# A recommendation kernel's first and last stretch: where rows are fetched, and which units run on column groups

## The chip, the core and the metric

The kernel runs on one core of a Trainium2 chip. A core has five engines that run side by side, each with its own queue of instructions: TensorE (PE, matrix products into PSUM), VectorE (DVE), ScalarE (ACT), GpSimd (POOL) and SyncE (SP, which only issues transfers). Transfers between the device's memory and the on-chip memory (SBUF) are DMAs; SP, ACT and POOL can issue them. The metric is the time of one execution in device microseconds, as the median of three runs. Before the change it is 31,195.79 us (31,191.82 to 31,199.41).

## What is computed

It is a recommender with attention over a history of 200 items for each of 16,384 users. Embedding rows have 64 floats (256 bytes), and the tables have 100,000 rows (users, items) and 1,000 (categories).

```python
u = u_emb[user]; it = i_emb[item]; c = c_emb[cate]
h = i_emb[hist]                                   # 200 x 16384 rows
itb = jnp.broadcast_to(it[None], h.shape)
feat = jnp.concatenate([h, itb, h - itb, h * itb], axis=-1)
a = dice(feat @ au_W1 + au_b1, au_alpha, axis=1)  # 36 units, statistics over the 16384 users
w = a @ au_W2 + au_b2
cur = jnp.sum(w * h, axis=0)
z = jnp.concatenate([u, it, c, cur], axis=-1)
z = dice(z @ W1 + b1, alpha1, axis=0)             # 80 units
z = dice(z @ W2 + b2, alpha2, axis=0)             # 40 units
return z @ W3 + b3                                # 2 outputs
# dice(x): p = sigmoid((x - mean) / sqrt(var + 1e-8)); x * (p + alpha * (1 - p))
```

The history's gather is the bulk: 3.28 million rows.

## The kernel before

The 16,384 users are 128 tiles of 128 (NT), in 8 chunks (ND) of 16 tiles (TD). One history position is therefore 8 steps, and the history 1,600 steps; `step(k)` does one. Five row buffers (`rows`, of 16 tiles each) are used in turn, so POOL may run up to five chunks ahead of DVE, which turns a buffer's rows into columns (`transpose`, L150, L153).

Rows come in one of two ways. `gather` (L124, L125) is an indirect DMA on POOL: one instruction fetches 128 rows by indices. Or "by address": SP or ACT loads row numbers, already multiplied to byte addresses (`load_addresses`, `scale_addresses`), into registers and issues one DMA of 256 bytes for each row (`ask`, L303 to L328, the DMA is L323). These rows land in `side`; `place_tile` (L385) waits for them (`await_rows`) and copies them into the chunk's last tile. Six of the eight chunks have such a tile (SIDES = 1, 3, 4, 5, 6, 7), which leaves 122 tiles to POOL; in two of three history positions chunk 5's is gathered as well.

There are three parts, each in an order written out by hand for every queue (`tc.manual_schedule`).

1. The start (L518 to L567). The items' rows are gathered by `fetch_all`, 122 tiles on POOL, and 768 rows come by address through `ask_all` (L541), 56% on SP and 44% on ACT. Beside it the categories' embeddings are made as a product with one-hot columns: ACT writes the category numbers in another order (`order_categories`, L487, L490), then spreads each half chunk over 125 partitions (`spread_categories`, L496); DVE compares them with eight constants (`pick_categories`, L501, 16 comparisons of 125x1024 a chunk), PE multiplies (L505, two column groups of 64), and ACT copies the product out (L509) and stores it (L516). Chunk 0 is followed by `attention_weights`. At the end of each chunk DVE places the chunk's last tile and transposes the chunk before. `head_weights` (L246 to L279) stands behind it all; of its SP transfers, seven are executed before the loop and the rest after it, as are the DVE operations L274 to L279 that use them.

2. The history: 180 positions in a hardware loop with a body of 90 (L570), then 20 more behind it (`steps`, L638). This part isn't touched.

3. The users' steps and the head (L645 to L675, then L677 to the end). In step j `fetch_all` gathers chunk j of the users' rows, SP loads the chunk's category columns from `catT` (L650), `step` finishes what is left of the history, and `ask_all` (L660) asks for a share of the users' rows by address, for five tiles, half on SP and half on ACT. For chunk c = j - 1 the first layer is computed by parts: category, item, attention (`head_layer`, L617), then the user part (L671) once the rows are transposed. Of the 80 units of this layer, 64 go into `px` with weights `w1a` (two halves of the users fill the 128 partitions), and the other 16 into `ph[:32]` with weights `w1b` (products of 128x32). ACT evacuates both (L623, L631), where L631 moves the 32 partitions to a quarter of `zb`, and `measure_head` (L581) takes statistics. After the last chunk the second layer runs chunk by chunk (L698 to L712): ACT and DVE apply dice, PE adds the product with `w2a` to that of the others with `w2b`, which is computed ahead for four chunks at a time in row groups of 32 (L705, `beside`). The third layer and the output follow.

ACT and SP execute their queues in order, so a row DMA that stands ahead of an activation delays it by its issue.

Of the kernel before, what the change touches and what calls it, by code (L numbers as in the profile page):

```python
# [14 lines left out]
P = 128  # L15
D = 64
# [20 lines left out]
def din_kernel(  # L37
# [76 lines left out]
    ids = [make(f"ids{i}", P, NC, dt=I32) for i in range(2)]  # L114
    side = [make(f"side{i}", P, D) for i in range(3)]
# [117 lines left out]
    w2b = make("w2b", P, P)  # L233
    w3 = make("w3", P, 4, P)
    b1a = make("b1a", P, 1)
    b1b = make("b1b", S, 1)
# [9 lines left out]
    def head_weights():  # L246
# [9 lines left out]
        for g in range(2):  # L256
# [6 lines left out]
            nc.sync.dma_start(b1b[ts(g, ZB)], col(b1)[ZA:])  # L263
            nc.sync.dma_start(bias2[g * ZA : g * ZA + Z2], col(b2))
            nc.sync.dma_start(al2[g * ZA : g * ZA + Z2], col(alpha2))
            for j in range(4):
                r = slice(j * S + g * ZB, j * S + (g + 1) * ZB)
                nc.sync.dma_start(w2b[r, g * ZA : g * ZA + Z2], W2[ZA:])
                w = j * S + g * ZO
                nc.sync.dma_start(w3[g * ZA : g * ZA + Z2, j, w : w + ZO], W3)  # L270
                nc.sync.dma_start(alb[r], col(alpha1)[ZA:])
        nc.sync.dma_start(bias3, b3.partition_broadcast(P))
# [64 lines left out]
    def ask_all(s, split, first, n, at, table):  # L337
        for queue, runs in enumerate(shares(NS * P // ND, s, split)):
            runs = [(r0, min(end, n * P)) for r0, end in runs if r0 < n * P]
            ask(queue, runs, first, range(n), at, table)  # L340

# [47 lines left out]
    def fetch_all(k, c, ids, table):  # L389
        for n in range(TD - (c in SIDES)):  # L390
            j = column(c, n)
            gather(rows[k % ROWS], ids[:, j : j + 1], n, table)
# [91 lines left out]
    def order_categories():  # L484
        for c in range(ND):
            n, j = TD - (c in SIDES), column(c, 0)
            nc.scalar.dma_start(cs[c][:, :n], columns(r_cate)[:, j : j + n])  # L487
            if c in SIDES:
                j = column(c, TD - 1)
                nc.scalar.dma_start(cs[c][:, n:], col(r_cate[j * P : (j + 1) * P]))  # L490
        nc.scalar.dma_start(table, c_emb.rearrange("(b p) d -> p b d", p=PB))
# [26 lines left out]
    with tc.manual_schedule():  # L518
        nc.sync.dma_start(ids[0], columns(r_item))
        load_addresses(2, r_item.rearrange("(o b) -> o b", o=1))  # L520
        nc.vector.memset(hm, 0.0)
        nc.scalar.copy(hT[SPREAD], hm)
        order_categories()
        load_hist_ids(0, 0)
        load_addresses(0, r_hist[0:1])
        nc.sync.dma_start(ids[1], columns(r_user))
        nc.gpsimd.iota(lanes, pattern=[[1, P]], base=P, channel_multiplier=-1)
        for q in range(SPREAD - 1):
            spread_categories(q)
# [4 lines left out]
        scale_addresses(2)  # L534
# [3 lines left out]
        for c in range(ND + 1):  # L538
            if c < ND:
                fetch_all(c, c, ids[0], i_emb)  # L540
                ask_all(c, 0.56, -NS, NS, addr[2], i_emb)  # L541
# [6 lines left out]
            if c == 0:  # L548
                attention_weights()
                scale_addresses(0)  # L550
            if c:
                if c - 1 in SIDES:
                    place_tile(c - 1, SIDES.index(c - 1) - NS)
                transpose(itT[c - 1], rows[(c - 1) % ROWS])
# [12 lines left out]
        head_weights()  # L567
# [10 lines left out]
    zst = [make(f"zst{i}", P, n, STATS) for i, n in enumerate((2 * ND, 4, 2 * ND))]  # L578

    def measure_head(i, j, t, h):  # L580
        nc.vector.bn_stats(zst[i][:, 2 * j + h, :], t[:, ts(h, CH)])  # L581

# [34 lines left out]
    def head_layer(pairs):  # L617
        layer(px, [(w1a[:, f], t) for f, t in pairs], last=False)
        layer(ph[:S], [(w1b[:, f], t) for f, t in pairs], last=False)
# [6 lines left out]
    def head_units(c):  # L626
# [3 lines left out]
        for h in range(2):  # L630
            nc.scalar.activation(  # L631
                zb[c // 4][ts(c % 4, S), ts(h, CH)], ph[:S, ts(h, CH)], AF.Identity, bias=b1b
            )
            if c % 4 == 3:
                measure_head(1, c // 4, zb[c // 4], h)

    with tc.manual_schedule():
        steps(BODY, L - BODY, L - BODY, r_user.rearrange("(o b) -> o b", o=1))  # L638
        U = addr[(L - BODY) % 3]
        j = column(SIDES[-1], TD - 1)  # L640
# [140 lines left out]
```

## Time and profile before

| what | value |
|---|---|
| median of three runs | 31,195.79 us |
| profiled execution | 31,199.79 us |
| its span | 31,198.0 us, 427,397 instructions |
| TensorE clock granted, mean | 0.809 |
| POOL busy | 23,418.8 us (75%), 24,783 instructions |
| PE busy | 20,922.2 us (67%) |
| DVE busy | 15,705.3 us (50%) |
| ACT busy | 3,823.8 us (12%) |
| POOL busy in 0 to 200, 200 to 400 us | 138.6 and 105.4 us |
| POOL busy in 1,000 to 5,000 us | 3,022.9 of 4,000 us |
| PE busy in 30,800 to 31,198 us | 297.0 of 398 us |
| by-address DMAs from the item table, SP and ACT | 68,720 and 68,624 |
| by-address DMAs from the user table, SP and ACT | 336 and 304 |

The span runs from the first to the last recorded instruction; the profiled execution is 1.8 us longer than its span and 4.0 us above the median. Busy time does not count the issue of a DMA by SP or ACT, nor the time between two gathers on POOL, so 75% is not a measure of how free POOL is. An engine's line in a timeline gives the start in us, the duration, the line of the kernel, the operation and its operands; "x16" means that so many like instructions are merged, and brackets hold the wait before the first of them and what ended it. "ACTq" and "SPq" are DMAs that these engines issue.

### The profile page before, as it was taken

What the parts mean: (1) busy time and instruction counts of PE and PEld (TensorE: products, weight loads), DVE (VectorE), ACT (ScalarE), POOL (GpSimd) and SP (SyncE); (2) the same over time, 40 slices, a digit from 0 to 9 for tenths busy, and PEclk for the clock granted to TensorE, in tenths of its full rate; (3) what the DMA queues carried; (4) which work ended last, traced back from release to release, by engine and by line L of the source; (5) the groups of instructions that cost most, each with busy time, mean ns of one, the idle gap of its engine ahead of it and who ended that gap; (6) DMA issues with size and microseconds to landing.
All of it is one profiled execution on the core that took longest, in us unless ns stands there. A gap on an engine that the chain in (4) does not pass through costs nothing.

```text
span 31198.0 us, 427397 instructions
## 1 busy us (share of the span) xinstructions
PE 20922.2 (67%) x39376; PEld 8551.5 (27%) x39376; DVE 15705.3 (50%) x21745; ACT 3823.8 (12%) x3330; POOL 23418.8 (75%) x24783
## 2 busy tenths in 40 slices
PE   5666666666666666666666666666666666666667
PEld 2222222222222222222222222222222222222222
DVE  4555554554555555555455455555555555545554
ACT  1111111111111111111111111111111111111111
POOL 6777777777777777777777777777777777777776
PEclk7888888888888888888888888887888888888888
DMA  2111111111111111111111111111111111111111
GB/s 41 29 29 29 29 29 29 29 29 29 29 29 29 29 29 29 29 29 29 29 29 29 29 29 29 29 29 29 29 29 29 29 29 29 29 29 29 29 29 30
DMA packets 1135469, 907.51 MB, mean 29 GB/s; under 512 B 730704, under 2 KB 730704, under 8 KB 1132426
## 3 DMA queue, kind: packets, MB, share of 16 engines
q0 software_dynamic: 792896, 813.51, 13.9%
q1 hardware_dynamic: 193404, 35.89, 0.8%
q10 hardware_dynamic: 146125, 30.64, 0.7%
q14 instruction: 2734, 22.39, 0.2%
q8 instruction: 310, 5.08, 0.1%
HBM read 873.55 MB, written 4.39 MB: 28 GB/s over the span
## 4 chain that ended last, share of the span: by engine, by line
POOL 32%; issue 12%; PE 5%; DMA 4%; DVE 2%; ACTq 1%; ACT 0%; DVEq 0%; POOLq 0%
POOL rows L125 32%; DMA rows<-in_L_rec_i_emb,idx 4%; PE px L158 2%; PE ph L158 1%; PE wb L158 1%; ACTq L323 1%; DVE hT L153 1%; DVE wb L368 0%; DVE curT L369 0%; ACT pg L361 0%; DVE st L377 0%; ACTq L315 0%; ACT xs L372 0%; DVE y L364 0%; DVE hm L400 0%
## 5 line engine op out<-in xcount | busy, mean ns | idle before, releaser
L125 POOL DMA_INDIRECT rows<-in_L_rec_i_emb,idx x24400 | 23038.6, 944 | 7542.4 <-issue 7198.7
L158 PE MATMUL ph<-hT,unit 128*128 128x512 f32 x6404 | 5928.7, 1077 | 9820.7 <-DVE hT L153 9820.2
L368 DVE SCALAR_TENSOR_TENSOR wb<-wb,au_bias,hT 128x1024 f32<-128x1024 f32 x1609 | 2080.3, 1293 | 9802.6 <-PE wb L158 9802.6
L158 PEld LDWEIGHTS ph<-hT,unit 128*128 128x128 f32 x6404 | 1747.3, 305 | 12865.9 <-DVE hT L153 12687.8
L153 DVE STREAM_TRANSPOSE hT<-rows 64x512 f32<-64x512 f32 x6404 | 4517.0, 705 | 1483.9 <-DMA rows<-in_L_rec_i_emb,idx 894.5
L158 PE MATMUL px<-hT,blk_h 128*128 128x512 f32 x6404 | 4125.0, 733 | 0.0
L372 ACT ACTIVATE xs<-px,au_bias 128x1024 f32<-128x1024 f32 x1602 | 1783.6, 1113 | 14375.2 <-PE wb L158 10720.9
L158 PE MATMUL wb<-y,blk_p 128*128 128x512 f32 x6436 | 3318.4, 597 | 246.6 <-DVE y L364 246.1
L361 ACT ACTIVATE pg<-xs,sh,rs 128x1024 f32<-128x1024 f32 x1609 | 1943.0, 1208 | 12481.6 <-issue 9985.6
L158 PE MATMUL px<-itT,blk_i 128*128 128x512 f32 x6404 | 3355.8, 606 | 0.0
L158 PE MATMUL wb<-xs,blk_x 128*128 128x512 f32 x6436 | 3300.5, 594 | 5.3 <-DVE curT L369 5.3
L158 PE MATMUL px<-hm,blk_m 128*128 128x512 f32 x6408 | 3011.2, 592 | 0.0
L400 DVE TENSOR_TENSOR hm<-ph,itT 128x1024 f32<-128x1024 f32 x1601 | 1960.6, 1225 | 1920.1 <-PE ph L158 1920.0
L364 DVE TENSOR_TENSOR y<-pg,xs 128x1024 f32<-128x1024 f32 x1609 | 1959.4, 1218 | 1293.7 <-ACT pg L361 1291.5
L158 PEld LDWEIGHTS px<-hT,blk_h 128*128 128x128 f32 x6404 | 1649.9, 258 | 2417.9 <-issue 2363.7
L377 DVE BATCH_NORM_STATS2 st<-xs 128x6 f32<-128x512 f32 x3204 | 2058.9, 685 | 60.8 <-ACT xs L372 17.1
L369 DVE TENSOR_TENSOR curT<-wb,curT 128x1024 f32<-128x1024 f32 x1609 | 1970.4, 1225 | 54.8
L158 PEld LDWEIGHTS px<-itT,blk_i 128*128 128x128 f32 x6404 | 1402.0, 219 | 2031.2 <-issue 2031.2
L158 PEld LDWEIGHTS wb<-y,blk_p 128*128 128x128 f32 x6436 | 1215.2, 191 | 1847.9 <-issue 1460.7
L158 PEld LDWEIGHTS wb<-xs,blk_x 128*128 128x128 f32 x6436 | 1224.6, 190 | 1551.9 <-issue 1544.4
L158 PEld LDWEIGHTS px<-hm,blk_m 128*128 128x128 f32 x6408 | 1217.4, 190 | 1532.9 <-issue 1520.3
L387 DVE COPY rows<-side 128x64 f32<-128x64 f32 x1079 | 235.7, 218 | 485.0 <-DMA side<-in_L_rec_i_emb 472.9
(184 smaller groups left out, 2044.3 us busy)
## 6 DMA issues: line engine op xcount, KB each, us to landing
side<-in_L_rec_i_emb SPq DMA_DIRECT2D x68720, 0.2 KB
side<-in_L_rec_i_emb ACTq DMA_DIRECT2D x68624, 0.2 KB
rows<-in_L_rec_i_emb,idx POOLq DMA_INDIRECT x24400
idx<-in_r_hist SPq DMA_DIRECT2D x200, 61.0 KB
hT<-cs ACTq DMA_DIRECT2D x16, 500.0 KB
side<-in_L_rec_u_emb SPq DMA_DIRECT2D x336, 0.2 KB
side<-in_L_rec_u_emb ACTq DMA_DIRECT2D x304, 0.2 KB
ucT<-catT SPq DMA_DIRECT2D x8, 512.0 KB
```

Of the source, the lines that this page charges most:

```text
L125: nc.gpsimd.indirect_dma_start(out=dst[:, n, :], out_offset=None, in_=table, in_offset=bass.IndirectOffsetOnAxis(ap=ids, axis=0),)
L153: nc.vector.transpose(by_tile(dst[ts(e, D)], i)[:, n], of[ts(i, D), n, ts(e, S)])
L158: nc.tensor.matmul(dst[:, ts(i, CH)], lhsT, rhs[:, ts(i, CH)], start=(first and j == 0), stop=(last and j == len(pairs) - 1), skip_group_c ...
L323: dma = issue.dma_start(side[m % 3].bitcast(U8)[p : p + 1], flat[ds(a, ROW)].rearrange("(o d) -> o d", o=1),).then_inc(landed[m % 3], 16)
L361: nc.scalar.activation(pg, xs[k % XR], AF.Sigmoid, bias=shifts[i], scale=rstds[i])
L364: nc.vector.tensor_mul(y, pg, xs[k % XR])
L368: nc.vector.scalar_tensor_tensor(wb, wb, au_bias2, hT[k % LAG], ALU.add, ALU.mult)
L369: nc.vector.tensor_add(curT[k % ND], wb, curT[k % ND])
L372: nc.scalar.activation(xs[k % XR], px, AF.Identity, bias=au_bias)
L377: nc.vector.bn_stats(stats[l % 3][:, 2 * c + i, :], xs[k % XR][:, ts(i, CH)])
L387: nc.vector.tensor_copy(rows[k % ROWS][:, TD - 1], side[m % 3])
L400: nc.vector.tensor_mul(hm, ph, itT[k % ND])
```

## The change

It has four parts.

- All 128 tiles of the items are gathered on POOL. The indices of the six tiles beyond the first 122 get a small tile of their own (`side_ids`, `load_all_ids`). `ask_all` is gone, and with it every by-address DMA of the start.
- ACT's order at the start is changed: the category numbers of three chunks, the table, and then the first spreads between the remaining numbers. `load_hist_ids` and `load_addresses` for the first position come behind `attention_weights`; the users' indices and `head_weights` are put into the third chunk.
- For the users, two tiles (of chunks 3 and 5) come by address, on SP alone, 48 rows a step; the other 126 are gathered. The category and item parts of the first layer are put ahead of a weighing.
- The 16 other units are computed for four quarters of the chunk's columns at once in PSUM, 256 columns each, one quarter for each group of 32 output columns; `zb` is then evacuated by one activation of 128x256, and measured for each chunk. In the second layer `w2b` has two copies, each with zeros for the other quarter, and the others' product of each chunk follows that with `w2a` in two row groups of 64. The bias `b1b` is loaded for all 128 partitions.

```diff
+    def load_all_ids(i, v):
+        for s in range(NS):
+            j = NC + s
+            nc.sync.dma_start(side_ids[i][:, s : s + 1], col(v[j * P : (j + 1) * P]))
-    def fetch_all(k, c, ids, table):
-        for n in range(TD - (c in SIDES)):
+    def fetch_all(k, c, i, table, by_address=()):
+        for n in range(TD):
             j = column(c, n)
-            gather(rows[k % ROWS], ids[:, j : j + 1], n, table)
+            at = ids[i][:, j : j + 1] if j < NC else side_ids[i][:, j - NC : j - NC + 1]
+            if j - NC not in by_address:
+                gather(rows[k % ROWS], at, n, table)
...
         nc.sync.dma_start(ids[0], columns(r_item))
-        load_addresses(2, r_item.rearrange("(o b) -> o b", o=1))
+        load_all_ids(0, r_item)
...
-        order_categories()
-        load_hist_ids(0, 0)
-        load_addresses(0, r_hist[0:1])
-        nc.sync.dma_start(ids[1], columns(r_user))
         nc.gpsimd.iota(lanes, pattern=[[1, P]], base=P, channel_multiplier=-1)
-        for q in range(SPREAD - 1):
-            spread_categories(q)
+        for c in range(3):
+            order_categories(c)
+        nc.scalar.dma_start(table, c_emb.rearrange("(b p) d -> p b d", p=PB))
+        for c in range(3, ND):
+            if c - 3 < SPREAD - 1:
+                spread_categories(c - 3)
+            order_categories(c)
...
-                fetch_all(c, c, ids[0], i_emb)
-                ask_all(c, 0.56, -NS, NS, addr[2], i_emb)
+                fetch_all(c, c, 0, i_emb)
...
             if c == 0:
                 attention_weights()
+                load_hist_ids(0, 0)
+                load_addresses(0, r_hist[0:1])
                 scale_addresses(0)
+            if c == 2:
+                nc.sync.dma_start(ids[1], columns(r_user))
+                load_all_ids(1, r_user)
+                head_weights()
             if c:
-                if c - 1 in SIDES:
-                    place_tile(c - 1, SIDES.index(c - 1) - NS)
                 transpose(itT[c - 1], rows[(c - 1) % ROWS])
...
-        head_weights()
...
+    def others(c):
+        return zb[c // 4][:, ts(c % 4, QH)]
-    def head_layer(pairs):
-        layer(px, [(w1a[:, f], t) for f, t in pairs], last=False)
-        layer(ph[:S], [(w1b[:, f], t) for f, t in pairs], last=False)
+    def head_layer(pairs, first=False, last=False, n=(0, TD)):
+        for i in range(2):
+            for j, (f, t) in enumerate(pairs):
+                nc.tensor.matmul(
+                    by_tile(px, i)[:, slice(*n)], w1a[:, f], by_tile(t, i)[:, slice(*n)],
+                    start=first and j == 0, stop=last, skip_group_check=True,
+                )
+        for j, (f, t) in enumerate(pairs):
+            for r in range(4):
+                n0 = r % 2 * TD // 2
+                of = slice(max(n[0], n0), min(n[1], n0 + TD // 2))
+                if of.start < of.stop:
+                    to = slice(of.start - n0, of.stop - n0)
+                    nc.tensor.matmul(
+                        ph[ts(r, S), :QH].rearrange("p (n t) -> p n t", t=S)[:, to],
+                        w1b[:, f], by_tile(t, r // 2)[:, of],
+                        start=first and j == 0, stop=last, skip_group_check=True,
+                    )
...
-        for h in range(2):
-            nc.scalar.activation(
-                zb[c // 4][ts(c % 4, S), ts(h, CH)], ph[:S, ts(h, CH)], AF.Identity, bias=b1b
-            )
-            if c % 4 == 3:
-                measure_head(1, c // 4, zb[c // 4], h)
+        nc.scalar.activation(others(c), ph[:, :QH], AF.Identity, bias=b1b)
+        nc.vector.bn_stats(zst[1][:, c, :], others(c))
...
+        tiles = [SIDES.index(c) for c in (3, 5)]
-        for j in range(ND + 2):
+        for j in range(ND + 1):
+            c = j - 1
             if j < ND:
-                fetch_all(K + j, j, ids[1], u_emb)
-                if j == SIDES[-1]:
-                    gather(rows[(K + j) % ROWS], sidx[0], TD - 1, u_emb)
+                fetch_all(K + j, j, 1, u_emb, tiles)
                 nc.sync.dma_start(category[j % 2], catT[j])
             step(K + j, K - 1, weighed)
             weighed.add(K + j - LAG)
+            runs = [(r0, r0 + LOAD) for r0 in (2 * LOAD * j, 2 * LOAD * j + LOAD)]
+            runs = [(r0, min(end, len(tiles) * P)) for r0, end in runs if r0 < len(tiles) * P]
+            ask(0, runs, first, tiles, U, u_emb)
+            if j:
+                head_layer(((2, category[c % 2]), (1, itT[c])), first=True)
...
-            if j < ND:
-                ask_all(j, SPLIT, first, NS - 1, U, u_emb)
-            if 1 <= j <= ND:
-                c = j - 1
-                head_layer(((2, category[c % 2]), (1, itT[c]), (3, curT[c])))
+            if j:
+                head_layer(((3, curT[c]),))
...
-                layer(pz[c % 4], [(w2a, curT[c])], first=False)
+                layer(pz[c % 4], [(w2a, curT[c])], last=False)
+                for r in (0, 2, 1, 3):
+                    of = ts(r // 2, D)
+                    nc.tensor.matmul(
+                        pz[c % 4][:, ts(r, QH)], w2b[of, r % 2], ab[c // 4][of, ts(c % 4, QH)],
+                        start=False, stop=r % 2 == 1, skip_group_check=True,
+                    )
```

## Prediction

> **What bounds the kernel now.** I read the page's groups first, then the timeline of GpSimd (POOL) from end to end, then the timelines of the other engines in the two stretches where POOL stands still or has finished. The group line gives engine, operation, tiles, count, then busy time and mean ns, then the idle time before them.
>
> ```profile
> L125 POOL DMA_INDIRECT rows<-in_L_rec_i_emb,idx x24400 | 23038.6, 944 | 7542.4 <-issue 7198.7
> ```
>
> Each gather takes 0.944 us, and nearly all of POOL's idle time is its own issue, 0.30 us a gather. The 24,778 starts lie 1.249 us apart on average, which makes 30,948 of the 31,198 us span. So the long middle is POOL's queue, which nothing in the change touches. Time can move only where POOL waits or after its last gather. In the timeline (start, us, engine, line, operation; in brackets the wait before it) the waits over 4 us are two at the start and one of 5.56 us at the loop's back edge:
>
> ```profile
> 177.08 0.94 POOL L125 DMA_INDIRECT rows<-in_L_rec_i_emb,ids  x1 [0.31 <-issue]
> 245.98 0.94 POOL L125 DMA_INDIRECT rows<-in_L_rec_i_emb,idx  x1 [67.96 <-DVE itT L153]
> 280.71 0.94 POOL L125 DMA_INDIRECT rows<-in_L_rec_i_emb,idx  x1 [14.82 <-DVE itT L153]
> 299.65 0.94 POOL L125 DMA_INDIRECT rows<-in_L_rec_i_emb,idx  x1 [0.52 <-DVE itT L153]
> ```
>
> POOL is through the items at 178 us, waits for the vector engine (DVE) to free row buffers, and from 299.65 (third history step) waits no more. What keeps DVE is on the scalar engine (ACT) and the tensor engine (PE):
>
> ```profile
> 97.95 19.47 ACTq L323 DMA_DIRECT2D side<-in_L_rec_i_emb  x42
> 117.52 0.58 ACT L509 COPY y<-pg 128x512 f32<-128x512 f32 x1 [25.38 <-issue]
> 118.15 8.80 PE L505 MATMUL pg<-xs,curT 125*64 125x512 f32 x32 [19.79 <-ACT y L509]
> ```
>
> ACT issues 42 row DMAs in 19.47 us before it copies the category product out, and PE stands 19.79 us for that copy. It repeats in all eight chunks, 35.5 us each. At the end POOL is not the bound:
>
> ```profile
> 31077.76 0.94 POOL L125 DMA_INDIRECT rows<-in_L_rec_u_emb,sidx  x1 [0.30 <-issue]
> 31045.93 1.26 ACT L623 ACTIVATE hT<-px,b1a 128x512 f32<-128x512 f32 x2 [17.06 <-issue]
> 31092.33 1.13 PE L158 MATMUL wb<-y,blk_p 128*128 128x512 f32 x2 [2.63 <-DVE y L364]
> 31107.44 1.90 PE L671 MATMUL ph<-ucT,w1b 128*32 128x512 f32 x4
> 31109.47 3.64 DVE L153 STREAM_TRANSPOSE ucT<-rows 64x384 f32<-64x384 f32 x8
> ```
>
> The last gather is issued at 31,077.76, yet its rows are transposed only at 31,109.47: the steps of the head, one every 20.7 us (the L623 evacuations start at 31,045.93, 31,066.46, 31,086.85), have fallen behind. PE works 18 of the 20.7 us, and ACT's 17 us of row DMAs make it as late.
>
> **Items gathered whole.** The 768 by-address rows of the start leave SP and ACT (eight times 42 on ACT); six gathers are added, 6 x 1.249 = 7.5 us, on POOL. A chunk then costs PE two runs of 7.03 us (the 126.79 us run of the same L505 shape) and a copy of about 0.9 with its waits, some 15 us; DVE 10.7 + 2.9 us; POOL 16 x 1.249 = 20 us. So POOL becomes the bound of the start, and only one thing delays it, the one-hot comparisons of DVE (L501), which run beside it:
>
> ```profile
> 53.49 11.31 POOL L125 DMA_INDIRECT rows<-in_L_rec_i_emb,ids  x1 [0.30 <-issue]
> 54.01 10.67 DVE L501 TENSOR_SCALAR xs<-hT,values 125x1024 f32<-125x1024 int32 x16
> ```
> ```profile
> 25.87 1.03 POOL L125 DMA_INDIRECT rows<-in_L_rec_i_emb,ids  x1 [0.30 <-issue]
> 22.61 11.73 DVE L501 TENSOR_SCALAR xs<-hT,values 125x1024 f32<-125x1024 int32 x16 [19.39 <-DMA hT<-cs]
> ```
> ```profile
> 90.15 1.41 POOL L125 DMA_INDIRECT rows<-in_L_rec_i_emb,ids  x1 [0.30 <-issue]
> ```
>
> One gather lasted 11.31 us, till the unbroken run of comparisons ended; in the first run gathers took 1.03; where DVE pauses for PE they take 1.41. Summed over the pitch, the five runs that met gathers cost POOL 1.6, 10.4, 4.1, 3.6 and 3.5 us. In the changed kernel all eight runs meet gathers: at the mean of these, 4.6, that is 37 us; the ends are 8 x 1.6 = 13 and 8 x 10.4 = 83. I take the mean, because the runs will be broken in part by a PE that starts each chunk at the slow clock. Then POOL reaches the third history step after 2.9 + 160 gathers x 1.249 + 37 = 240 us instead of 299.65: a gain of 60 us (84 to 14).
>
> The Trainium skill, "SBUF — State Buffer", section "SBUF: two separate sides", speaks against this part: a DVE operation in a two-port mode holds the port it shares with GpSimd for the whole instruction, and GpSimd cannot write descriptors meanwhile, while DMAs issued from SP or ACT are immune. The 11.31 us gather agrees with it, the 1.03 us ones do not; by the rule alone all runs would cost the 10.4 us end, and the start would gain 14 us.
>
> **Constants and spread numbers early.** The spread's first DMA is issued some 7 us sooner; that brings DVE forward, not POOL: nothing. The head's weights (L247 on) move from behind the start, where most were issued after the loop, into the third chunk. There DVE waits for them:
>
> ```profile
> 27876.84 0.15 DVE L274 TENSOR_SCALAR al1a<-ala 128x1 f32<-128x1 f32 x1 [13.45 <-DMA ala<-in_L_rec_alpha]
> 27857.47 0.94 POOL L125 DMA_INDIRECT rows<-in_L_rec_i_emb,idx  x1 [2.86 <-DVE rows L387]
> ```
>
> At the loop's end DVE loses 13.45 + 4.93 us to them, but POOL no more than 2.86, which is the loop's own barrier: five row buffers hide it, so removing it gains nothing (at most 2.6). In the third chunk SP issues 63 DMAs instead; 49 took 25.3 us at the loop's end, so 33 us in which DVE stands, with PE and the transposes queued behind it. Cover: DVE's chunk of 13.6 us against POOL's 24.6. DVE is released near 22 + 3 x 13.6 + 16 (attention weights, 34 to 54 us now, partly waits) + 33 = 112 us; POOL needs that row buffer for its seventh chunk at 3 + 6 x 24.6 = 151. Nothing, then; without the 39 us cover it would cost up to 33. The first history numbers move behind the attention weights in SP's queue; they are needed near 190 us: nothing.
>
> **The users' steps.** 304 rows leave ACT; SP keeps 256, 48 a step at 17.6 us, in steps of about 20 us, and the first tile placed (chunk 3) has two steps of slack. The gathers become 126 instead of 123: the last starts 125 x 1.249 = 156 us after the first user gather (30,925.42 in the trace; times below count from it), its rows are usable 2.7 to 4.3 us later (the gather at 27,816.22 was transposed at 27,818.93, the one at 30,924.17 at 30,928.42), so at 160.
>
> The 16 units beyond 64 ("others") now run as four column groups of 256 columns. Before: 8 matmuls of 512 columns, 0.86 us each (the starts of consecutive ones), 6.9 us a chunk. The trace has no four-group matmul; the nearest row is L505, two groups of 64 columns, whose 16 matmuls of 512 columns took 7.03 us, 0.44 each, half of 0.86. Ends: four at once, 1.7 us a chunk; one after another, 6.9. I take 1.7, as both groups of the row overlap wholly. A step is then: evacuation 1.3, category and item products 4.3 (ACT's gate and DVE's product beside them), attention sums 3.4, DVE's weighing 2.5, transposes 2.9, user product 1.8, and waits of 0.5: 16.7 us, under POOL's 20. Chunk 0 is transposed at 35 now, chunk 1 (with a second weighing) at 67; I put chunk 1 at 60, and chunk 7 at 60 + 5 x 16.7 + 9 (no gate in it) = 153, before its rows. So POOL sets the end: 160 + 1.2 for the last transposes, then the 75.2 us that follow the last part's product (31,122.78 to 31,198): 237. Before it was 272.6. Gain 35; with groups one after another chunk 7 stays near its 184 and the gain is about 3. That is the range of this part.
>
> The Trainium skill, "TensorEngine Tiling (Array Packing)", section "Tiling Modes", says that a change of tiling mode drains the engine, which speaks against groups between full products; the row has no such change, and the page gives no price, so no other sum follows.
>
> In the second layer 8 x 4 matmuls of 256 columns in two row groups replace 16 of 512: at 0.43 a pair 6.9 us against 5.1, under ACT's 29 us; the first starts 2 us later on a slow clock (+0.9), the shorter statistics of the others save 0.9: nothing, within 1 us either way.
>
> **Sum.** 60 + 35 = 95 off a span of 31,198.0 (the profiled execution took 31,199.8, 4.0 above the median of 31,195.8): 31,101 for the median.
>
> **The rivals.** (a) Lock-out: every comparison run shuts POOL out as at 53.49. Gain 14 + 35 = 49, 31,147. For: runs unbroken by ACT's waits. Against: four of five rows. (b) The groups run one after another: 60 + 3, 31,133. For: the four share one bank. Against: L505. Both together: 31,179. (c) Slower: each group matmul pays for a change of mode. From where it decides: the step must reach 29.9 us for chunk 7 to lie 60 us behind today's 184, thus 16 groups in 14.9 us, 0.93 each instead of 0.11. At 1.2, what a slow-clock record of L705 (32x512) takes, the step is 34 us and the end 31,226. Against: L671 changes between 128 and 32 columns now, 1.90 after 1.98, without a visible gap. (d) The change does not do what it says: the SP rows come a step late, 20 us, 31,121; inside the range.
>
> **Chances.** Forecast 0.74 (own range 31,075, with 13 us of lock, to 31,130), (a) 0.12, (b) 0.07, both 0.03, (c) 0.04. The range 31,075 to 31,150 leaves out (c), both, and a little at the lower end. A measurement tells 0.2%, 62 us, from no change. Faster: the forecast and half of (b), 0.78. Within: (a), half of (b), both, 0.18. Slower: 0.04.
>
> **What would show it.** First history gather near 200 us (not 246), no POOL wait over 4 us before 300, gathers of 1.4 to 11 us beside L501 in all chunks; a 33 us DVE wait at the constants; no such wait at the loop's end; four group matmuls inside 0.5 us; users' evacuations 20 us apart; 120 us from the last gather to the end now, 81 then. Wrong if a POOL wait takes the place of the two, or if the evacuations stay 20.7 us apart with PE busy.

## The result and the profile after

The changed kernel takes 31,084.69 us (median of 6 runs), the kernel before 31,196.67 (6 runs beside it): a ratio of 0.9967, 95% interval 0.9956 to 0.9978, or 112 us less. The forecast was 31,101 with a range of 31,075 to 31,150. The profiled execution of the changed kernel took 31,151.97 us, 67 more than the median, while its five other runs lie between 31,080.4 and 31,086.5; where the 67 us are is shown first, because every line below comes from that execution.

The group of the history gathers on the page of the changed kernel (engine, operation, tiles, count; busy time and mean ns; idle time before):

```profile
L126 POOL DMA_INDIRECT rows<-in_L_rec_i_emb,idx x24400 | 23097.4, 947 | 7463.6 <-issue 7179.4
```

A gather lasts 946.6 ns here against 944.2 before, and the mean distance of two starts is 1.2525 us against 1.2499. The change does not touch the loop. 24,500 gathers of it times 2.6 ns are 64 us: this execution ran its long middle at a slower beat. The first user gather therefore starts only 12 us earlier than before (30,913.53 for 30,925.42). The start and the tail have to be compared each in itself.

The start, from the timelines of POOL, DVE, ACT and PE of the changed kernel (start, us, engine, line, operation, count, in brackets the wait before it and what ended it):

```profile
18.03 1.02 POOL L126 DMA_INDIRECT rows<-in_L_rec_i_emb,ids  x1 [0.30 <-issue]
44.61 11.49 POOL L126 DMA_INDIRECT rows<-in_L_rec_i_emb,ids  x1 [0.30 <-issue]
119.56 1.41 POOL L126 DMA_INDIRECT rows<-in_L_rec_i_emb,ids  x1 [0.30 <-issue]
186.09 0.94 POOL L126 DMA_INDIRECT rows<-in_L_rec_i_emb,idx  x1 [0.30 <-issue]
...
44.01 0.68 DVE L146 TENSOR_SCALAR addrs<-addrs 1x768 int32<-1x768 int32 x1 [2.62 <-DMA addrs<-in_r_hist]
44.61 10.67 DVE L502 TENSOR_SCALAR xs<-hT,values 125x1024 f32<-125x1024 int32 x16
97.87 0.15 DVE L275 TENSOR_SCALAR al1a<-ala 128x1 f32<-128x1 f32 x1 [27.43 <-DMA bias<-in_L_rec_b]
104.49 0.15 DVE L275 TENSOR_SCALAR al1b<-alb 128x1 f32<-128x1 f32 x1 [6.46 <-DMA alb<-in_L_rec_alpha]
...
134.73 0.59 ACT L510 COPY y<-px 128x512 f32<-128x512 f32 x1 [6.28 <-PE px L506]
135.37 7.09 PE L506 MATMUL px<-xs,curT 125*64 125x512 f32 x32 [0.69 <-ACT y L510]
```

ACT now copies a category product out as soon as PE has made it, and PE stands 0.69 us for the copy, where it stood 19.79 behind the row DMAs. The runs of comparisons of chunks 4 to 7 start 14.6 us apart, so DVE and PE are faster than POOL's 20 us a chunk.

The waits of 68 and 15 us are gone; POOL goes from its last item gather to the first history gather (186.09, before 245.98) with 0.30 us between. The third history step (the 32nd history gather) starts at 224.9 us instead of 299.65: 74.8 us gained. One gather is again shut out for 11.5 us, from the moment at which it starts together with the second run of comparisons. The constants hold DVE for 27.43 + 6.46 = 33.9 us, and POOL waits for nothing meanwhile.

The tail, same kernel, timelines of POOL, ACT, PE and DVE:

```profile
31069.89 0.95 POOL L126 DMA_INDIRECT rows<-in_L_rec_u_emb,side_ids  x1 [0.30 <-issue]
...
31045.92 1.27 ACT L647 ACTIVATE hT<-px,b1a 128x512 f32<-128x512 f32 x2 [14.64 <-PE px L629]
31063.16 1.27 ACT L647 ACTIVATE hT<-px,b1a 128x512 f32<-128x512 f32 x2 [14.51 <-PE px L629]
31074.40 1.27 ACT L647 ACTIVATE hT<-px,b1a 128x512 f32<-128x512 f32 x2 [9.60 <-PE px L629]
...
30966.38 0.64 PE L639 MATMUL ph<-ucT,w1b 128*32 128x256 f32 x8
30966.84 0.61 PE L639 MATMUL ph<-itT,w1b 128*32 128x256 f32 x8
30967.38 1.13 PE L159 MATMUL wb<-xs,blk_x 128*128 128x512 f32 x2
...
31067.46 2.35 DVE L154 STREAM_TRANSPOSE ucT<-rows 64x384 f32<-64x384 f32 x4 [1.97 <-DMA rows<-in_L_rec_u_emb,ids]
31072.37 1.28 DVE L154 STREAM_TRANSPOSE ucT<-rows 64x128 f32<-64x128 f32 x4 [2.56 <-DMA rows<-in_L_rec_u_emb,side_ids]
```

The last rows are now transposed 2.48 us after the last gather starts, and DVE waits for the DMA that brings them: the chain of the head has caught up. Counted from the first user gather, the last gather starts at 156.4, its transposition at 158.8, and the span ends at 236.7; before, the end was at 272.6. So the tail gained 35.9 us. From the last gather to the end it is 80.3 us, before 120.2. Start and tail, 74.8 + 35.9 = 110.7, agree with the 112 us of the medians. (The trace holds two records for each of these matmuls, so "x8" in a row of group matmuls is four of them.)

### The profile page after: what moved, and what is told of

The parts are those of the page before. It is cut to its first block, busy times and chain, and to the rows that moved or that the text cites. A ratio compares the mean times of both kernels' runs of the same rounds, so it can differ in the third digit from the quotient of the medians.

```text
span 31150.2 us, 425358 instructions
## 1 busy us (share of the span) xinstructions
PE 20932.5 (67%) x39536; PEld 8562.0 (27%) x39536; DVE 15693.7 (50%) x21739; ACT 3818.6 (12%) x3322; POOL 23487.0 (75%) x24792
## 3 DMA queue, kind: packets, MB, share of 16 engines
q0 software_dynamic: 793184, 813.81, 11.9%
## 4 chain that ended last, share of the span: by engine, by line
POOL 29%; issue 11%; PE 7%; DMA 3%; DVE 3%; ACTq 2%; ACT 0%; DVEq 0%; POOLq 0%
POOL rows L126 29%; PE px L159 3%; DMA rows<-in_L_rec_i_emb,idx 3%; PE ph L159 2%; PE wb L159 2%; ACTq L324 1%; DVE hT L154 1%; DVE wb L364 1%; DMA rows<-in_L_rec_i_emb,sidx 0%; DVE curT L365 0%; DVE st L373 0%; ACT pg L357 0%; ACT xs L368 0%; ACTq L316 0%; DVE mv L409 0%
```

## The experiments

There were twelve runs of eight kernels (e4b, e5b, e6b and e6d repeat a kernel), and only two of them, e5b and e6b, were on a chip where the kernel before took its time (31,203 us). The other ten were on three other chips, where the kernel before took 50,723 to 51,190 us; what differed there is shown under e1. Their ratios hold for that condition alone.

**e5 and e5b: the other units as before.** The changed kernel with the old form of the 16 units beyond 64, in both layers.

```diff
+        for out, w in ((px, w1a), (ph[:S], w1b)):
+            for i in range(2):
+                for j, (f, t) in enumerate(pairs):
                     nc.tensor.matmul(
-                        ph[ts(r, S), :QH].rearrange("p (n t) -> p n t", t=S)[:, to],
-                        w1b[:, f], by_tile(t, r // 2)[:, of],
+                        by_tile(out, i)[:, slice(*n)], w[:, f], by_tile(t, i)[:, slice(*n)],
...
```

> The changed kernel, but the 16 other units as before: 32 columns for 512 items, 8 matmuls a chunk one after another, and 16 of 512 in the second layer. The two tiles by address on SyncE stay. Theory (column groups needed): a step of 17.2 us grows by the 6.9 - 1.7 = 5.2 us of PE to 22.4, above POOL's 20, and the last chunk is late by about 32 us: about 31,116, and 105 to 115 us from the last gather to the end. Rival (ACT's row DMAs alone were the cause): the steps stay under 20 us, 80 us from the last gather to the end, 31,085.

> The kernel of the earlier run with the 16 other units as before, once more, since that run and the kernel before beside it took over 50,500 us. Where the kernel before takes its 31,197 us again: theory (column groups needed), the users' steps grow from 17.2 to about 22.4 us, the last chunk comes some 32 us late, about 31,116, with 105 to 115 us from the last gather to the end. Rival (ACT's row DMAs alone were the cause): steps under 20 us, 80 us from the last gather to the end, 31,085.

e5 had 50,585.93 us beside 50,723.24 (0.9970, 0.9959 to 0.9980) and tells nothing of this by its total. e5b: 31,104.92 us, ratio 0.9968 (0.9956 to 0.9981). Its timelines of ACT, PE and DVE at the end:

```profile
30974.39 1.26 ACT L637 ACTIVATE hT<-px,b1a 128x512 f32<-128x512 f32 x2 [15.03 <-PE px L630]
30993.82 1.27 ACT L637 ACTIVATE hT<-px,b1a 128x512 f32<-128x512 f32 x2 [15.20 <-PE px L630]
31013.03 1.27 ACT L637 ACTIVATE hT<-px,b1a 128x512 f32<-128x512 f32 x2 [15.03 <-PE px L630]
...
31018.39 1.04 PE L630 MATMUL ph<-ucT,w1b 128*32 128x512 f32 x2
31029.22 0.62 PE L630 MATMUL ph<-ucT,w1b 128*32 128x128 f32 x4
...
31014.95 3.64 DVE L154 STREAM_TRANSPOSE ucT<-rows 64x384 f32<-64x384 f32 x8
```

The steps are 19.3 us apart, not 17.2 and not 22.4. The last chunk's rows are transposed in one group of eight at 31,014.95, without a wait for a DMA, so they were there; what is late is PE, whose last product starts at 31,029.22, 184.1 us after the first user gather (30,845.13). The end follows 258.6 us after that gather, between the 272.6 before and the 236.7 of the change. From the last gather to the end it is 102.5 us. Hence of the tail's 35.9 us the column groups bring 21.9, and 14.0 come without them. The medians give the groups 20.2 us as they stand (31,104.92 less 31,084.69) and 13.9 if each is taken against the kernel before beside it (gains of 98.1 and 112.0), so their part is 14 to 22 us. The part without them holds the rows that left ACT and the category and item products put ahead of a weighing; no run has the one without the other on this chip. Both theories were off: without the groups the tail did not get as short, and the groups were not the whole of it.

**e6 and e6b: rows back on ACT, column groups kept.** Five user tiles by address, half of their rows on ACT. They stand ahead of the gate of the step, which the expectations did not take into account; in the kernel before they follow its weighing.

```diff
-        tiles = [SIDES.index(c) for c in (3, 5)]
+        tiles = list(range(NS - 1))
...
-            ask(0, runs, first, tiles, U, u_emb)
+            if j < ND:
+                ask_all(j, SPLIT, first, NS - 1, U, u_emb)
             if j:
                 head_layer(((2, category[c % 2]), (1, itT[c])), first=True)
...
                 gate(left[0])
```

> The changed kernel with its column groups, but five of the users' tiles by address as before, half of their rows on ACT (40 DMAs a step in about 17 us), so 3 gathers fewer. Theory (ACT's rows make a step as late as PE did): ACT's step is 17 + gate 1.1 + evacuations 1.8 = about 20 us and the chain catches up nothing, 31,100 to 31,115. Rival (PE's column groups alone suffice): the chain still reaches the last rows on time, and three gathers fewer make it 31,081.

> The kernel of the earlier run with five of the users' tiles by address, half of their rows on ACT, column groups kept, once more for the same reason. Where the kernel before takes its 31,197 us again: theory (ACT's rows make a step as late as PE did), ACT's step is 17 + 1.1 + 1.8 = about 20 us, the chain catches up nothing, 31,100 to 31,115. Rival (column groups alone suffice): the chain reaches the last rows on time and three gathers fewer make it 31,081.

e6 had 50,648.84 beside 50,723.24 us (0.9985, 0.9976 to 0.9994). e6b: 31,155.68 us, ratio 0.9985 (0.9976 to 0.9995), 71 us more than the changed kernel and far above both expectations. Its timelines of ACT and PE:

```profile
30956.08 1.27 ACT L652 ACTIVATE hT<-px,b1a 128x512 f32<-128x512 f32 x2 [13.39 <-PE px L634]
30958.55 17.88 ACTq L324 DMA_DIRECT2D side<-in_L_rec_u_emb  x48
30976.48 1.21 ACT L362 ACTIVATE pg<-xs,sh,rs 128x1024 f32<-128x1024 f32 x1 [18.77 <-issue]
30991.15 1.27 ACT L652 ACTIVATE hT<-px,b1a 128x512 f32<-128x512 f32 x2 [13.46 <-PE px L634]
...
30979.00 2.08 PE L159 MATMUL wb<-y,blk_p 128*128 128x512 f32 x2 [15.85 <-DVE y L365]
```

ACT issues 48 row DMAs in 17.88 us, and only then the gate, on which DVE's product and PE's attention sums wait: PE stands 15.85 us in this step, and the evacuations are 35 us apart (30,956.08 and 30,991.15), as in three more steps. The span ends 308.7 us after the first user gather, 72 later than in the changed kernel, which is the whole 71 us. So what ACT's rows cost depends on what stands behind them in ACT's queue: with them ahead of the gate a step takes 35 us; before the change, with them behind the weighing, it took 20.4 to 22.4. The next kernel puts them where the kernel before has them.

**e6c and e6d: the same rows behind the weighing.** The edit is shown against e6.

```diff
-            if j < ND:
-                ask_all(j, SPLIT, first, NS - 1, U, u_emb)
             if j:
                 head_layer(((2, category[c % 2]), (1, itT[c])), first=True)
...
                 weighed.add(left[0])
+            if j < ND:
+                ask_all(j, SPLIT, first, NS - 1, U, u_emb)
```

> As the last run (five of the users' tiles by address, half of their rows on ACT, column groups kept), but each step's rows are issued after its gate and weighing, where the kernel before has them, and not ahead of the gate, where they held the gate up for 17.9 us and PE for 15.9 us. Theory: the rows lie beside PE's products again; ACT's step is 1.2 + 17.5 + 1.8 = 20.5 us against 17.2, so the chain catches up nothing: some 20 us lost, less three gathers (3.75 us), about 31,100. Rival one (the rows are hidden altogether beside PE): 31,081. Rival two (the rows cost as much as in the last run wherever they stand): 31,155.

> The kernel of the earlier run with five of the users' tiles by address, half of their rows on ACT after each step's gate and weighing, once more for the same reason. Where the kernel before takes its 31,200 us again: theory (the rows lie beside PE's products, ACT's step is 1.2 + 17.5 + 1.8 = 20.5 us against 17.2), some 20 us lost less three gathers (3.75 us), about 31,100. Rival one (the rows are hidden altogether): 31,081. Rival two (they cost as much as ahead of the gate): 31,155.

Both ran on the other chips: 50,660.51 beside 50,848.68 us (0.9964, 0.9951 to 0.9978) and 51,058.32 beside 51,190.19 (0.9971, 0.9960 to 0.9981). The totals do not tell the three expectations apart. The tails do, one trace each: from the first user gather to the end it is 411.1 us in e6c, where e3, e4 and e7 on the same chip, with the changed kernel's tail, need 396.7 to 400.2; 417.2 in e6d beside 400.9 in e4b; but 471.3 in e6, with the rows ahead of the gate, beside 397.0 in e2. So behind the weighing the rows lose 11 to 16 us there, near the theory's 16 (20 less 3.75) and not rival one's gain of 4, and ahead of the gate 74. Rival two falls, under that condition. On the first chip the price in that place was not measured.

**e1 and e2: the start alone, the tail alone.** e1 is the changed kernel with the users' steps and the head of the kernel before; e2 is the other half. The excerpts are against the changed kernel.

```diff
# e1, the users' steps
-                fetch_all(K + j, j, 1, u_emb, tiles)
+                fetch_all(K + j, j, 1, u_emb, range(NS - 1))
...
+                ask_all(j, SPLIT, first, NS - 1, U, u_emb)
# e2, the start
-                fetch_all(c, c, 0, i_emb)
+                fetch_all(c, c, 0, i_emb, range(NS))
+                ask_all(c, 0.56, -NS, NS, addr[2], i_emb)
```

> The start as changed (items gathered whole, constants early), the users' steps and the head as before. Theory: the start and the tail add, so this kernel gains what POOL gains at the start, the third history step at 226 us instead of 299.65: 73 us off 31,197, about 31,123; the last gather stays some 120 us before the end. Rival one: the start's gain is partly eaten later, since the users' chain is as late as it is whenever the gathers end; then under 50 us, above 31,147. Rival two: the tail gains nothing of its own and the start makes the whole difference, about 31,085.

> The start as before, only the users' steps and the head as changed. Theory: the third history step stays near 300 us, the last gather moves from 120 us before the end to 80, less 3 more gathers (3.75 us): a gain of 36 us, about 31,161. Rival: the tail gains nothing of its own, 31,197; or the head's early constants are needed for it to gain (they are late here), then between 31,165 and 31,195.

Beside a kernel before of 50,723.24 us (50,635.61 to 50,796.03), e1 took 50,614.27 (0.9976, 0.9966 to 0.9986) and e2 50,682.96 (0.9992, 0.9983 to 1.0001). Here the loop is not POOL's. From e1's timelines of ACT and POOL in the loop:

```profile
1004.14 31.62 ACTq L324 DMA_DIRECT2D side<-in_L_rec_i_emb  x20
1035.81 1.21 ACT L362 ACTIVATE pg<-xs,sh,rs 128x1024 f32<-128x1024 f32 x1 [32.13 <-issue]
1037.46 6.64 ACTq L324 DMA_DIRECT2D side<-in_L_rec_i_emb  x20
...
1051.90 0.95 POOL L126 DMA_INDIRECT rows<-in_L_rec_i_emb,idx  x1 [20.45 <-DVE hT L154]
```

Twenty row DMAs of ACT take 31.62 us, and the next twenty 6.64. In the slow stretches the single instructions of ACT's and SP's queues, register moves included, mostly stand 0.70 us apart or a multiple of it; the gate (L362) starts only behind the 31.62 us, and POOL waits 20.45 us for row buffers (1,345 such waits on DVE, 19,166 us in all). The gathers themselves keep their beat (1.252 us median). So their totals cannot price a step of the forecast, which rests on POOL's queue. What they show is weaker: the start alone and the tail alone add up, 0.9976 and 0.9992 (an interval that holds 1) giving 0.9968, where the kernels that hold both parts had 0.9964 to 0.9972, e6 with its rows ahead of the gate left out. Counted from the first user gather e1 needs 425.9 us and e2 397.0, so the changed tail gains 29 us there, for 35.9 on the first chip. The 81 us by which e1's first history gather comes ahead of e2's (250.4 and 331.7) have the sign of the change's 60, with other waits in it.

**e3: the constants in the last chunk of the start.**

```diff
-            if c == 2:
+            if c == 7:
                 nc.sync.dma_start(ids[1], columns(r_user))
                 load_all_ids(1, r_user)
                 head_weights()
```

> The changed kernel, but the head's constants and the users' numbers are loaded in the last chunk of the start, not in the third. Theory: DVE stands the same 33 us there, near 190 us; the item rows it holds up are needed by POOL only at about 246 us, after a transposition at about 220, so nothing is lost: 31,085, no POOL wait over 4 us before 300. Rival (the cover is gone): a POOL wait of up to 33 us near 250, up to 31,118.

50,669.27 us beside 50,848.68 (0.9967, 0.9954 to 0.9981). The total tells nothing, but the traces do, since on these chips DVE had fallen behind already in the first chunk (five waits of some 10 us in the first run of comparisons) and the cover was gone. First e4 (same chip, constants in the third chunk), then e3:

```profile
172.80 0.15 DVE L275 TENSOR_SCALAR al1a<-ala 128x1 f32<-128x1 f32 x1 [28.64 <-DMA bias<-in_L_rec_b]
184.38 1.34 POOL L126 DMA_INDIRECT rows<-in_L_rec_i_emb,ids  x1 [31.74 <-DVE itT L154]
...
241.05 0.15 DVE L275 TENSOR_SCALAR al1a<-ala 128x1 f32<-128x1 f32 x1 [22.20 <-DMA bias<-in_L_rec_b]
252.57 0.94 POOL L126 DMA_INDIRECT rows<-in_L_rec_i_emb,idx  x1 [25.28 <-DVE itT L154]
```

In e4 DVE stands for the constants until 179.5 us, transposes right behind them, and POOL waits 31.74 us for that; e3 has no such wait there, and its last item gather starts at 201.3 us instead of 228.0. So without the cover the constants cost POOL 31.7 us in the third chunk. In e3 DVE stands until 247.7, and POOL waits 25.28 us for the transposes behind that, the rival's sign; but e4 waits near there too (21.57 us to 250.82, behind comparisons that go at PE's pace), so what the constants add in the last chunk is not shown. On the first chip the third chunk's cover held; whether it reaches to the last chunk there was not measured.

**e4 and e4b: the address scaling moved away from the second run of comparisons.**

```diff
             if c == 0:
                 attention_weights()
                 load_hist_ids(0, 0)
                 load_addresses(0, r_hist[0:1])
-                scale_addresses(0)
...
+            if c == 4:
+                scale_addresses(0)
```

> The changed kernel, but DVE scales the first history step's addresses after the fifth chunk's comparisons, not just ahead of the second run of them. In both traces the one gather that lasts over 11 us lies beside the run that follows this scaling at once. Theory one (the scaling just ahead sets it off): no gather over 1.5 us at the start, the first history gather at 176 us instead of 186, 31,075. Theory two (chance of phase: a gather that starts together with an unbroken run of comparisons is shut out to its end): a long gather shows again at this or another run, 186 us, 31,085.

> The kernel of the earlier run that scales the first history step's addresses after the fifth chunk's comparisons, once more, since the kernel before took over 50,800 us beside that run. Where the kernel before takes its 31,200 us again: theory one (the scaling just ahead of the second run of comparisons sets the long gather off), no gather over 1.5 us at the start, the first history gather at 176 us instead of 186, 31,075. Theory two (phase: a gather that starts together with an unbroken run is shut out to the run's end), a long gather shows at this or another run, 186 us, 31,085.

50,663.23 beside 50,848.68 us (0.9967, 0.9954 to 0.9979), and 51,061.47 beside 51,190.19 (0.9972, 0.9962 to 0.9983). Neither has the long gather, but neither could have: the second run of comparisons began only at 117.2 us, while POOL stood waiting (from 104.8 us in e4, 103.9 in e4b), as it did in e1 with the scaling in its old place. The experiment failed for want of a gather beside that run. What stands is an observation: in all five traces where a gather met that run directly behind the scaling (before, after, e5b, e6b, e7), it was shut out to the run's end, for 11.3 to 11.9 us and in e7 for 19.1; no other unbroken run with gathers beside it did this. The traces also answer theory two. From e6b, the second run, the operation ahead of it, and the gathers that meet the starts of the second and the third run:

```profile
44.07 11.88 POOL L126 DMA_INDIRECT rows<-in_L_rec_i_emb,ids  x1 [0.30 <-issue]
57.51 1.31 POOL L126 DMA_INDIRECT rows<-in_L_rec_i_emb,ids  x1 [0.30 <-issue]
...
43.99 0.54 DVE L146 TENSOR_SCALAR addrs<-addrs 1x768 int32<-1x768 int32 x1
44.46 10.67 DVE L507 TENSOR_SCALAR xs<-hT,values 125x1024 f32<-125x1024 int32 x16
```

The third run starts at 57.95. So one gather began 0.39 us ahead of its run and was shut out, the other 0.44 ahead and lasted 1.31. Over the five traces the gathers shut out began 0 to 0.51 us ahead of their run, and others that began 0.22 to 0.44 us ahead of theirs lasted 0.94 to 1.31. The start relative to the run does not decide, then; all five began while the scaling still ran, which ends 0.07 us into the run. How the scaling, or an operation of its kind directly ahead, would do this is open.

**e7: the comparisons as TENSOR_TENSOR.** The same ones come out.

```diff
-            nc.vector.tensor_scalar(
-                ones, spread[q % SPREAD], values[:PB, b : b + 1], None, ALU.is_equal
+            nc.vector.tensor_tensor(
+                ones, spread[q % SPREAD], values[:PB, b : b + 1].to_broadcast([PB, CD]), ALU.is_equal
             )
```

> The changed kernel with the comparisons of the start written as TENSOR_TENSOR against a broadcast value; the same ones come out. If such an operation lasts 1.2 us for 1024 elements, as TENSOR_TENSOR of 128x1024 does elsewhere in this kernel, a chunk takes DVE 16 x 1.2 + 2.9 = 22 us against POOL's 20. Theory (the mode of TENSOR_SCALAR is what delays the gathers): gathers beside it keep their 0.944 us, the 23 us of delay go, the first history gather starts at 163 us; DVE has fallen some 50 us behind by its 8 chunks and the constants, less than the five row buffers' 100 us, so 31,062. Rival one (any DVE work beside a gather delays it): 186 us, 31,085. Rival two (DVE becomes the bound): a POOL wait between 180 and 300 us, above 31,085.

50,688.32 us beside 50,848.68 (0.9971, 0.9960 to 0.9982). The total is one of the other chips', but in its first 90 us POOL never waits longer than its own 0.30 us between gathers, and its timelines there can be read:

```profile
16.85 0.94 POOL L126 DMA_INDIRECT rows<-in_L_rec_i_emb,ids  x1 [0.30 <-issue]
20.27 1.97 POOL L126 DMA_INDIRECT rows<-in_L_rec_i_emb,ids  x1 [0.30 <-issue]
22.54 1.97 POOL L126 DMA_INDIRECT rows<-in_L_rec_i_emb,ids  x1 [0.31 <-issue]
36.16 0.94 POOL L126 DMA_INDIRECT rows<-in_L_rec_i_emb,ids  x1 [0.30 <-issue]
44.90 19.06 POOL L126 DMA_INDIRECT rows<-in_L_rec_i_emb,ids  x1 [0.30 <-issue]
...
17.92 18.26 DVE L502 TENSOR_TENSOR xs<-hT,values 125x1024 f32<-125x1024 int32 x16 [15.53 <-issue]
44.26 0.70 DVE L146 TENSOR_SCALAR addrs<-addrs 1x768 int32<-1x768 int32 x1
44.90 18.23 DVE L502 TENSOR_TENSOR xs<-hT,values 125x1024 f32<-125x1024 int32 x16
```

The theory fell: the gathers beside TENSOR_TENSOR last 1.97 us, not 0.94, more than beside TENSOR_SCALAR (1.02). The starts lie 2.27 us apart, and 18.26 us over 16 comparisons is 1.14: a gather with its issue takes the time of two comparisons. The same holds in the changed kernel: two of 0.662 us make the 1.325 beside an unbroken run, two of 0.858 (where DVE goes at PE's pace) the 1.717. Nor is it any DVE work: in the loop of the changed kernel 604 gathers between 5,000 and 8,000 us began inside a DVE operation of over 0.8 us (hm, y, wb and curT, each with one operand in PSUM), and those lasted 946 to 949 ns on average and none over 1.12 us. The loop's transposes and statistics, which read SBUF alone, leave gathers at 946 ns too. So rival one falls as well. The sign of rival two came, two POOL waits of 12.2 and 31.2 us that end at 193.7 and 256.9 us, but waits of that size stand in every run on these chips, so it is not tested.

## Why the prediction was right

**POOL bounds the kernel, and time moves only at the two ends: right.** The gain is the 74.8 us up to the third history step and the 35.9 after the first user gather. No POOL wait over 4 us is left before 300 us. At the loop's end two starts lie 4.24 us apart, before 3.81, though DVE no longer waits for constants: its removal there gained nothing, as costed.

**Items gathered whole: right in mechanism, the lock term mis-sized.** PE's wait for ACT's copy went from 19.79 to 0.69 us and POOL became the bound of the start, as forecast; no run takes the row DMAs away without the new order of ACT's loads. The term "at the mean of these, 4.6, that is 37 us" was too large. The eight runs cost POOL 1.5, 10.5, 1.0, 1.3, 2.1, 2.1, 2.1 and 2.1, together 22.8 us. The error is in how the choice was argued, "because the runs will be broken in part by a PE that starts each chunk at the slow clock": apart from the one run in which a gather is shut out, pauses make a run dearer, not cheaper. Where comparisons follow one another a gather takes two of 0.662 us and loses 0.07; where they are paced by PE it takes two of 0.858 and loses 0.47. The 3.5 to 4.1 us runs of the kernel before were the slow, broken ones (L501 spread over 14.5 to 15.8 us); the changed kernel's runs hold nine or more comparisons in a row some 0.66 us apart. The one dear run of 10.4 us should have been counted once, for the second run again, and the others by their pace, not all by one mean. That is 14.2 of the 14.8 us by which the start gained more than the 60 forecast. Another 1.2 come from the count: 159 gathers stand ahead of the third history step, not 160 (chunk 1 of the history has 15). The slower beat of the traced execution takes 0.6 back.

The page rule weighed there (the Trainium skill, "SBUF — State Buffer", section "SBUF: two separate sides") says that the loser is shut out for the whole DVE instruction, and the forecast read it as the whole run. The traces agree with the rule as it is written, instruction by instruction: beside unbroken comparisons a gather takes two of them, start to start, and not the run, except in the one run, which the rule does not explain. The same section names DVE operations with two SBUF inputs beside the two-port modes (against a GpSimd operation that reads SBUF, as these gathers do with their indices), and so does "GPSIMD Engine Reference", section "1. Specifications"; e7 (1.97 us) and the loop's operations with a PSUM operand (946 to 949 ns) agree with that.

**Constants early: right.** 33 us were forecast as DVE's wait, 33.9 came, and POOL did not feel it. Without the cover the forecast had up to 33 us; on another chip, where it was gone, POOL waited 31.7 (e4).

**Users' steps: right in sum, and partly for reasons that were sized wrongly.** 156, 160 and 237 us were forecast for the last gather, its rows and the end; 156.4, 158.8 and 236.7 came. Four group matmuls take 0.46 us (30,966.38 to 30,966.84), the step is 17.1 us on average for a forecast 16.7. The transposes of the last chunk start at 153.9 us, forecast 153, and wait 1.97 us for rows already then; the last rows came at 158.8. So POOL set the end, and errors in the step had no effect on it. One was large: the groups were to save 5.2 us of a step (6.9 less 1.7), and against e5b PE's busy time in a step fell by 4.0 (18.4 to 14.5) and the step by 2.2 (19.3 to 17.1). The granted clock was 1.00 in e5b's steps and 0.89 to 0.97 in these. The mark "evacuations 20 us apart" was wrong: the chain falls behind in its first chunks, runs at its own 17 us, and meets POOL's 20 only at the last chunk. Rival (b) was given a gain of 3 us with the groups one after another; e5b has 14.0, since its chain ran at 19.3 us a step, where 16.7 and 5.2 make 21.9. Rival (c), a dear change of tiling mode, is excluded by the 0.46 us. From the last part's product to the end it took 1.3 us more (76.5 for 75.2), just outside the 1 us either way given to the second layer.

**What else made up the number.** 95 us forecast, 112 measured: 14.8 from the start, 0.9 from the tail, the remaining 1.3 within the spread of the runs (some 5 us on either side). No errors cancelled between the two parts: both came out above the forecast.

## What to carry to other kernels

Where one queue holds most of the span, cost a change at its two ends only, and check there which engine ends the last wait. Before putting rows on an engine's DMA queue, look at what stands behind them: here forty-eight DMAs ahead of one short activation made a step 35 us long instead of 17, and behind it, on other chips, they cost 11 to 16 us in all. When work is moved under the cover of buffers, ask what is left of it when the engine behind is late: 33.9 us were hidden on one chip, and 31.7 showed on another. Where gathers on GpSimd run beside DVE work, look at which operations stretch them: here the comparisons did, to two instructions a gather and once to the whole run, and operations with one operand in PSUM, transposes and statistics did not.

## What the runs showed that was not expected

The beat of the gathers is not a constant of the kernel. 944 ns and 1.249 us apart in the traces of before, e5b and e6b; 946.6 and 1.252 in that of the changed kernel, and both kinds among the other chips' runs (943.4 in e4b's loop, 946.0 in e4's). It holds through a whole execution and is worth 64 us here, more than half of the change's gain; what sets it is open.

On three other chips the same kernel before took 50,723, 50,849 and 51,190 us for 31,200. ACT and SP issued in steps of 0.70 us through long stretches, the granted TensorE clock was 0.70 instead of 0.81, and POOL, bound by its own queue on the first chip, waited for row buffers on these. The changed kernel itself did not run there; the kernels that hold both parts still gained (0.9964 to 0.9972; e6, with its rows ahead of the gate, 0.9985). Why the queues issue so slowly there was not tried.
